# Choosing 128 of 4096 tokens for each of 48 experts: one wide search, or many short ones and a second one over their results

## The chip, the cores and the metric

The kernel runs on one core of a Trainium2 chip. The metric is the device time of one execution in microseconds (us), as the median of several runs. The core has five engines that work side by side and wait for each other through semaphores: TensorE (matrix products, PE in the profile), VectorE (DVE), ScalarE (ACT), GpSimd (POOL) and SyncE (SP). SP issues most transfers between main memory and the on-chip memory; GpSimd issues those whose rows are given by a list of indices.

## The reference

The program is a chain of four blocks over 16 sequences of 256 tokens, 128 numbers each (4096 tokens, float32). Every block is half a feed-forward step, an attention step and the same half feed-forward step again, each on the layer-normed input and added to x. The change concerns the feed-forward step of block 2, a mixture of experts in which the experts choose tokens:

```python
def _L2_ffn_ref(x, Wr, W1, b1, W2, b2):
    CAP_FACTOR = 1.5
    ...
    cap = int(CAP_FACTOR * T / E)            # 128 tokens for each of E = 48 experts
    logits = xf @ Wr.T                       # T = 4096
    vals, idx = jax.lax.top_k(logits.T, cap)
    w = jax.nn.softmax(vals, axis=-1)
    xg = xf[idx]
    h = jax.nn.gelu(jnp.einsum('ecd,esdm->ecsm', xg, W1) + b1[:, None], approximate=False)
    y = jnp.einsum('ecsm,esmk->ecsk', h, W2) + b2[:, None]
    y = y.reshape(E, cap, D) * w[..., None]
    out = jnp.zeros_like(xf).at[idx.reshape(-1)].add(y.reshape(-1, D))
    return out.reshape(orig_shape)
```

So each expert takes the 128 tokens with its highest logits, weights them by a softmax over these 128 values, and adds its results to the tokens' rows. The step runs twice, before and after the attention of block 2.

## The kernel before

The list `steps` at the end of `macaron_kernel` runs twelve steps in order: ffn0, attn0, ffn0, ffn1, attn1, ffn1, ffn2, attn2, ffn2, ffn3, attn3, ffn3. x, its normed copy xn (tokens on partitions) and the transposed normed copy xnT stay on chip throughout. A framework orders the instructions of a step by its own estimate of when each is ready, by program order among those that are, and may take an instruction early into the step before. Two things limit that. `pin` ties an instruction to the last pinned one on the same engine, so that pinned instructions of an engine keep program order. An `If` on a value read from memory is a unit: nothing moves into it, out of it or across it.

**Pieces.** `norm_piece(c)` (through `roots`) norms 512 tokens: statistics and an inverse root in some 22 small VectorE operations, then four ScalarE activations that write xn. `turn_piece(c)` transposes these four tiles on TensorE and copies them into xnT. Both are pinned. The plain `layernorm` does all of x at once without pins.

**ffn2.** It stores xn to `xn_dram` for the gathers, clears one accumulator in main memory and stores x to the other. The router product (L1275) puts the logits of 64 experts (48 real) on partitions 0 to 63 for tokens 0 to 2047 and on 64 to 127 for the rest, 2048 to a partition. The search (L1282 to L1286) makes 16 rounds: MAX8 finds the eight highest of a row, FIND_INDEX8 their places, MATCH_REPLACE8 overwrites them. `expert_lists` turns the lists of both halves so that slots lie on partitions; half 1 is reversed, so that a comparison slot by slot (L1294) leaves the best 128. Softmax weights follow (L1304 to L1315).

The expert loop then takes each of the 48 experts: GpSimd gathers 128 rows of 512 bytes into xg (L1328, three buffers), TensorE transposes (L1335), VectorE copies (L1337), four products h (L1340), four Gelu activations (L1344), the bias and four products y (L1346, L1348), the weighting into ys (L1352), and a scatter that adds ys to the accumulator (L1353). Weights come on SP for four experts at a time. `gather_acc` sums the accumulators into x.

**ffn1**, 64 experts with eight per token, comes before the first ffn2. Its second call has `normed=True`. After its own routing and search it reads a flag under an `If` (L1068, L1069), then loops over eight groups of eight experts; each group has four gathers (L1087) and four scatters (L1127) on GpSimd. Six of the groups also call `shared(c)`, which completes x for 512 tokens that no expert can touch unless the flag is set. Only the first 1024 tokens' x waits for `gather_acc`, and a second `If` (L1135) follows it. In the first call `norm_piece` and `turn_piece` of the six later pieces run inside this loop.

**attn2** is a pipeline written out by hand over 22 values of s, nearly all pinned, one sequence per s. In a step come `keys(s)` (L1421), `rest(s-2)` (L1570), `renorm` in odd steps, `stand` (L1481, and L1484 on VectorE), `through` (L1496), `divisors` (L1515), `queries`, `divide`, `gather`, `put(s-1)` (L1559) and norm pieces. The results of `gather`'s totals, `stand` and `put` share one memory bank, the pool `pm` with one buffer.

Of the kernel before, what the change touches and what calls it, by code (L numbers as in the profile page):

```python
# [9 lines left out]
F32 = mybir.dt.float32  # L10
# [30 lines left out]
GE2 = 4  # L41

# [28 lines left out]
def macaron_kernel(ctx: ExitStack, tc: tile.TileContext, I: dict, out: bass.AP):  # L71
# [93 lines left out]
    def iota(name, pattern, base, mult, n):  # L165
        t = const.tile([P, n], F32, name=name)
        G.iota(t, pattern=pattern, base=base, channel_multiplier=mult, allow_small_or_imprecise_dtypes=True)
        return t
# [21 lines left out]

    left = iota("left", [[-P, NT]], T, -1, NT)
# [14 lines left out]
    xn_dram = dram.tile([T + PAD, D], F32, name="xn_dram")  # L206

# [3 lines left out]
    SP.dma_start(out=xn_dram[T:, :], in_=zeros[:, :D])  # L211
    for a in acc:
        SP.dma_start(out=a[T:, :], in_=zeros[:, :D])
# [84 lines left out]
    def norm_piece(c):  # L298

        t0 = 4 * c  # L300
        less, r = roots(x[:, t0 : t0 + 4, :], LN_EPS)
        for j in range(4):
            pin(
                S.activation(  # L304
                    xn[:, t0 + j, :], x[:, t0 + j, :], AF.Identity, bias=less[:, j : j + 1], scale=r[:, j : j + 1]
                )
            )
# [606 lines left out]
    def ffn1(call, normed):  # L914
# [8 lines left out]
        with tc.tile_pool(name=f"f1r{call}", bufs=1) as rp, tc.tile_pool(name=f"f1w{call}", bufs=2) as wp, tc.tile_pool(  # L923
# [148 lines left out]
            with tc.tile_pool(name=f"f1h{call}", bufs=1, space=PSUM) as ph:  # L1072
                n = GE1 // 2
                for g in range(E1 // GE1):

                    if g < NT // 4 - FIRST // 4:
                        c = FIRST // 4 + g
                        if not normed:
                            norm_piece(c)
                            turn_piece(c)  # L1080
                        shared(c, ph)
                    wgu, wd = early.pop(g, None) or weights(g)
# [51 lines left out]
            gather_acc(acc, 0, FIRST)  # L1134
            rv = nc.values_load(more[0:1, 0:1], min_val=0, max_val=P * E1)  # L1135
            with tc.If(rv > 0):
                gather_acc(acc, FIRST, NT, add=True)

# [119 lines left out]
    def ffn2(call, normed):  # L1258
        if not normed:
            layernorm()  # L1260
        SP.dma_start(out=xn_dram[:T, :].rearrange("(j p) d -> p j d", p=P), in_=xn)
# [4 lines left out]
        with tc.tile_pool(name=f"f2r{call}", bufs=1) as rp, tc.tile_pool(name=f"f2w{call}", bufs=2) as wp, tc.tile_pool(  # L1266
            name=f"f2t{call}", bufs=3
        ) as tp3:
            lgT = rp.tile([P, T // 2], F32, name="f2_lgT")
            with tc.tile_pool(name=f"f2p{call}", bufs=2, space=PSUM) as pr:  # L1270
                for c in range(4):
                    lp = pr.tile([P, 512], F32, tag="lp", name="f2_lp")
                    for h in range(2):
                        t0 = h * (T // 2) + c * 512
                        PE.matmul(  # L1275
                            lp[64 * h : 64 * h + 64, :], W["f2_rw"], xnT[:, t0 : t0 + 512], start=True, stop=True
                        )
                    S.copy(lgT[:, c * 512 : (c + 1) * 512], lp)
            vals = rp.tile([P, CAP2], F32, name="f2_vals")
            where = rp.tile([P, CAP2], U32, name="f2_where")  # L1280
            for r in range(CAP2 // 8):
                cut = slice(8 * r, 8 * r + 8)  # L1282
                V.max(out=vals[:, cut], in_=lgT)  # L1283
                V.max_index(out=where[:, cut], in_max=vals[:, cut], in_values=lgT)  # L1284
                if r < CAP2 // 8 - 1:
                    V.match_replace(out=lgT, in_to_replace=vals[:, cut], in_values=lgT, imm_value=LOWEST)  # L1286
            wf = rp.tile([P, CAP2], F32, name="f2_wf")
            V.tensor_copy(wf, where)
            V.tensor_scalar(wf[64:P, :], wf[64:P, :], float(T // 2), None, ALU.add)
            lv = expert_lists(vals, "f2v")  # L1290
            li = expert_lists(wf, "f2i")

            pick = rp.tile([P, 64], F32, name="f2_pick")
            V.tensor_tensor(pick, lv[:, :64], lv[:, 64:], ALU.is_ge)  # L1294
            top = rp.tile([P, 64], F32, name="f2_top")
            V.tensor_tensor(top, lv[:, :64], lv[:, 64:], ALU.max)
            tokf = rp.tile([P, 64], F32, name="f2_tokf")
            V.tensor_tensor(tokf, li[:, :64], li[:, 64:], ALU.subtract)
            V.tensor_tensor(tokf, tokf, pick, ALU.mult)
            idx = rp.tile([P, 64], I32, name="f2_idx")  # L1300
            V.tensor_tensor(idx, tokf, li[:, 64:], ALU.add)  # L1301

            tpa = pst.tile([P, 512], F32, tag="tp", name="f2_tpa")
            PE.transpose(tpa[:64, :P], top, ident)  # L1304
            nm = rp.tile([64, 1], F32, name="f2_nm")
            V.tensor_reduce(nm, tpa[:64, :P], AX.X, ALU.max, negate=True)
            ex = rp.tile([64, P], F32, name="f2_ex")
            sm = rp.tile([64, 1], F32, name="f2_sm")
            S.activation(ex, tpa[:64, :P], AF.Exp, bias=nm, accum_out=sm)
            V.reciprocal(sm, sm)  # L1310
            V.tensor_scalar(ex, ex, sm, 0.5, ALU.mult, ALU.mult)
            tpb = pst.tile([P, 512], F32, tag="tp", name="f2_tpb")
            PE.transpose(tpb[:, :64], ex, ident[:64, :64])
            wgt = rp.tile([P, 64], F32, name="f2_wgt")
            V.tensor_copy(wgt, tpb[:, :64])  # L1315

            with tc.tile_pool(name=f"f2h{call}", bufs=2, space=PSUM) as ph:
                for g in range(E2 // GE2):
                    w1 = wp.tile([P, GE2, S2, M2], F32, tag="w1", name="f2_w1")
                    SP.dma_start(out=w1.rearrange("p e s m -> p (e s m)"), in_=I["f2_w1"][g])  # L1320
                    w2 = wp.tile([P, GE2, S2, K2], F32, tag="w2", name="f2_w2")
                    SP.dma_start(out=w2.rearrange("p e s k -> p (e s k)"), in_=I["f2_w2"][g])
                    b2 = wp.tile([1, GE2, D], F32, tag="b2", name="f2_b2")
                    SP.dma_start(out=b2.rearrange("p e d -> p (e d)"), in_=I["f2_b2"][g : g + 1, :])
                    for i in range(GE2):
                        e = g * GE2 + i
                        xg = tp3.tile([P, D], F32, tag="xg", name="f2_xg")
# [3 lines left out]
                            in_=xn_dram,  # L1331
# [3 lines left out]
                        PE.transpose(tp[:, :P], xg, ident)  # L1335
# [16 lines left out]
                        V.tensor_scalar(ys, y, wgt[:, e : e + 1], None, ALU.mult)  # L1352
# [10 lines left out]
    def attn2():  # L1363

        NP2 = H2 // 2
        with tc.tile_pool(name="a2", bufs=2) as ap, tc.tile_pool(name="a2w", bufs=1) as wp, tc.tile_pool(
# [219 lines left out]
            for s in range(BATCH + 6):  # L1586
# [24 lines left out]
                if s >= 5 and s % 2 and (s - 5) // 2 < pieces:  # L1611
                    norm_piece((s - 5) // 2)


    def ffn3(call, last):
# [176 lines left out]
        lambda: ffn2(0, False), attn2, lambda: ffn2(1, True),  # L1792
        lambda: ffn3(0, False), attn3, lambda: ffn3(1, True),
    ]
    banks = None
    for step in steps:
        if step in (attn0, attn3):
            if banks is not None:
                banks.close()
                banks = None  # L1800
            if step is attn3:
                late_pool.append(ctx.enter_context(tc.tile_pool(name="late", bufs=2)))
            step()
        else:
            if banks is None:
                banks = ExitStack()
                pst.pool, pst.tag = banks.enter_context(tc.tile_pool(name="pst", bufs=2, space=PSUM)), "tp"
            step()
    banks.close()
# [90 lines left out]
```

## Time and profile before

| | |
|---|---|
| median of 3 runs | 3072.5 us (3072.13 to 3077.36) |
| the profiled execution | 3084.44 us, span 3082.7 us |
| TensorE, VectorE, ScalarE, GpSimd busy | 2349.2, 1567.7, 1002.9, 758.2 us |
| mean granted TensorE clock | 0.841 |
| first ffn2: x complete, search, first gather, last scatter | 1168.8; 1194.0 to 1305.4; 1309.0; 1475.2 us |
| attn2: last output product ends | 1843.1 us |
| second ffn2: search, last scatter | 1868.1 to 1979.5; 2147.8 us |
| ffn1, second call: first gather, last scatter | 1044.5; 1152.8 us |

A group line reads: line, engine, operation, out<-in, shapes, count, busy us, mean ns, and the idle time of that engine just before with what ended it. A time-line row begins with its start and duration. A row of a table by stretches gives, for each engine, busy us and instructions, then the granted clock as a share of full speed, the busy share of the transfer engines and GB/s. An `f_` in a name stands for any of the prefixes f0_ to f3_.

### The profile page before, as it was taken

The page shows a single profiled execution, that of the slowest core. Times are in us where ns is not written, and L with a number is a line of the kernel's source. Part 1 is how long each engine was busy: PE and PEld are TensorE (multiplying, and loading weights), DVE is VectorE, ACT ScalarE, POOL GpSimd, SP SyncE. Part 2 cuts the span into 40 slices and gives each one's busy share as a digit, 9 for nine tenths or more (in the row PEclk, how much of TensorE's full clock was granted, in tenths as well). Part 3 has the DMA queues.
Part 4 walks back from the last instruction along what each step waited for, and adds up shares of the span by engine and source line. Part 5 has one row for each costly group of instructions (what it writes and reads, how often), then busy time and mean ns, then how long its engine had stood idle before and what let it go on. Part 6 is the DMA issues. An engine that isn't in the chain of part 4 may idle for free.

```text
span 3082.7 us, 44329 instructions
## 1 busy us (share of the span) xinstructions
PE 2349.2 (76%) x16626; PEld 1776.8 (58%) x16626; DVE 1567.7 (51%) x3989; ACT 1002.9 (33%) x2211; POOL 758.2 (25%) x673
## 2 busy tenths in 40 slices
PE   5885896883745561099799981298899989999999
PEld 4773555772545350088566650187588745556887
DVE  5336664336447527911245449711555566653553
ACT  1222221221225201033444531033444445654443
POOL 1550000551630270067100001176111100002111
PEclk9997886995869765567899995567999989999999
DMA  4842232453530354045300002055100022220000
GB/s 138 257 136 63 79 100 76 148 150 88 134 67 8 95 108 142 0 119 128 89 1 1 1 1 89 26 125 128 30 1 1 2 43 59 61 63 13 8 11 11
DMA packets 197271, 215.68 MB, mean 70 GB/s; under 512 B 37329, under 2 KB 162290, under 8 KB 193682
## 3 DMA queue, kind: packets, MB, share of 16 engines
q1 hardware_dynamic: 161978, 177.63, 19.0%
q0 software_dynamic: 35072, 35.16, 6.8%
q8 instruction: 133, 2.18, 0.3%
q14 instruction: 88, 0.72, 0.1%
HBM read 142.76 MB, written 61.31 MB: 66 GB/s over the span
## 4 chain that ended last, share of the span: by engine, by line
PE 46%; DVE 10%; DMA 2%; ACT 1%; issue 1%; POOL 1%; another core or an unknown queue 0%; POOLq 0%; DVEq 0%; ACTq 0%; SPq 0%
PE f_m L1683 12%; PE f_h L1340 4%; PE a_s L822 4%; PE f_y L1348 2%; DVE f_where L1284 2%; DVE f_vals L1283 2%; DVE f_lgT L1286 2%; PE a_po L564 2%; PE a_t L822 2%; PE a_op L1559 2%; PE a_gp L1469 2%; PE f_yp L1741 2%; PE a_qp L1432 2%; PE a_kp L1421 2%; PE f_z L1663 2%; PE f_z L1664 2%
## 5 line engine op out<-in xcount | busy, mean ns | idle before, releaser
L471 PE MATMUL f_h<-f_xsT,f_w 128*128 128x256 f32 x736 | 189.8, 396 | 34.4 <-ACT f_sg L473 27.7
L826 DVE TENSOR_REDUCE a_nm<-a_s 128x4 f32<-128x1024 f32 x128 | 156.3, 1224 | 100.4 <-PE a_t L822 89.1
L304 ACT ACTIVATE xn<-x,ln_less,ln_r 128x128 f32<-128x128 f32 x256 | 105.8, 482 | 290.7 <-DVE ln_less L295 280.2
L445 POOL DMA_INDIRECT f_xs<-xn_dram,f_src x92 | 90.6, 985 | 371.1 <-DVE f_past L418 290.2
L474 DVE SCALAR_TENSOR_TENSOR f_hs<-f_h,f_b1s,f_sg 128x256 f32<-128x256 f32 x184 | 88.1, 482 | 180.3 <-issue 97.3
L822 PE MATMUL a_t<-a_q,a_k 32*128 32x256 f32 x1024 | 173.3, 424 | 3.5 <-ACT a_e L830 3.5
L1344 ACT ACTIVATE f_hs<-f_h,w_f_b 128x128 f32<-128x128 f32 x384 | 109.6, 369 | 203.0 <-PE f_h L1340 172.4
L830 ACT ACTIVATE a_e<-a_t 128x512 f32<-128x512 f32 x256 | 139.1, 594 | 104.5 <-PE a_t L822 104.5
L1328 POOL DMA_INDIRECT f_xg<-xn_dram,f_idx x96 | 96.5, 1005 | 304.0 <-DVE f_idx L1301 257.4
L471 PEld LDWEIGHTS f_h<-f_xsT,f_w 128*128 128x128 f32 x736 | 134.0, 197 | 62.5 <-ACT f_sg L473 34.4
L1340 PE MATMUL f_h<-f_xgT,f_w 128*128 128x128 f32 x768 | 165.7, 364 | 0.0
L896 PE MATMUL f2v_tp<-ident,f2v_turned 128*128 128x128 f32 x2 | 0.9, 475 | 212.2 <-DVE f2v_turned L893 212.2
L1352 DVE TENSOR_SCALAR f_ys<-f_y,f_wgt 128x128 f32<-128x128 f32 x96 | 33.6, 350 | 250.5 <-PE f_y L1348 182.2
L1353 POOL DMA_INDIRECT acc<-f_ys,f_idx x96 | 150.8, 1571 | 40.0 <-issue 24.0
L822 PE MATMUL a_s<-a_k,a_q 32*128 32x256 f32 x1024 | 155.2, 431 | 2.3 <-DVE a_nm L826 1.6
L473 ACT ACTIVATE f_sg<-f_h,f_b1s 128x256 f32<-128x256 f32 x184 | 84.9, 474 | 214.5 <-PE f_h L471 182.2
L1348 PEld LDWEIGHTS f_y<-f_w,f_hs 128*128 128x128 f32 x768 | 139.6, 238 | 15.9 <-ACT f_hs L1344 4.3
L1348 PE MATMUL f_y<-f_w,f_hs 128*128 128x32 f32 x768 | 146.0, 290 | 2.1 <-ACT f_hs L1344 2.0
L312 PE MATMUL ln_tp<-ident,xn 128*128 128x128 f32 x256 | 56.0, 321 | 111.7 <-ACT xn L304 101.1
L1340 PEld LDWEIGHTS f_h<-f_xgT,f_w 128*128 128x128 f32 x768 | 136.7, 257 | 0.7 <-issue 0.4
L1702 ACT ACTIVATE f_nh<-f_c,w_f_sh 128x256 f32<-128x256 f32 x192 | 86.9, 500 | 127.7 <-DVE f_c L1721 103.2
L896 PEld LDWEIGHTS f2v_tp<-ident,f2v_turned 128*128 128x128 f32 x2 | 0.4, 182 | 212.7 <-DVE f2v_turned L893 212.7
(398 smaller groups left out, 5756.0 us busy)
## 6 DMA issues: line engine op xcount, KB each, us to landing
f_w<-in_f_w SPq DMA_DIRECT2D x24, 1024.0 KB
f_w<-in_f_w SPq DMA_DIRECT2D x46, 512.0 KB
f_w<-in_f_w SPq DMA_DIRECT2D x70, 256.0 KB
a_ud<-a_u SPq DMA_DIRECT2D x32, 512.0 KB
f_wgu<-in_f_wgu SPq DMA_DIRECT2D x16, 768.0 KB
acc<-zeros SPq DMA_DIRECT2D x14, 512.0 KB
acc_t<-acc SPq DMA_DIRECT2D x14, 512.0 KB
f_wd<-in_f_wd SPq DMA_DIRECT2D x16, 384.0 KB
```

Of the source, the lines that this page charges most:

```text
L304: S.activation(xn[:, t0 + j, :], x[:, t0 + j, :], AF.Identity, bias=less[:, j : j + 1], scale=r[:, j : j + 1])
L445: G.indirect_dma_start(out=xs[:, i, :], out_offset=None, in_=xn_dram, in_offset=bass.IndirectOffsetOnAxis(ap=src[:, s : s + 1], axis=0),)
L471: pin(PE.matmul(h[:, k, :], w1[:, cc * P : (cc + 1) * P], xsT, start=True, stop=True))
L822: pin(PE.matmul(ps[:, c, :], sta[:, c * P : (c + 1) * P], mov, start=True, stop=True))
L826: pin(V.tensor_reduce(m, sp, AX.X, ALU.max, negate=True))
L830: pin(S.activation(e, tp, AF.Exp, scale=scale))
L1328: G.indirect_dma_start(out=xg, out_offset=None, in_=xn_dram, in_offset=bass.IndirectOffsetOnAxis(ap=idx[:, e : e + 1], axis=0),)
L1340: PE.matmul(h[:, s, :], w1[:, i, s, :], xgT, start=True, stop=True)
L1344: S.activation(hs[:, s, :], h[:, s, :], AF.Gelu, bias=W["f2_b1"][:, col : col + 1])
L1348: PE.matmul(y[:, s * K2 : (s + 1) * K2], hs[:, s, :], w2[:, i, s, :], start=False, stop=(s == S2 - 1))
L1353: G.indirect_dma_start(out=acc2[e % 2], out_offset=bass.IndirectOffsetOnAxis(ap=idx[:, e : e + 1], axis=0), in_=ys, in_offset=None, comput ...
L1683: PE.matmul(dst[:, n, :], sta[:, k, n * P : (n + 1) * P], mov[:, k, :], start=first and n == 0 and k == 0, stop=n == 1 and k == 1, skip_gr ...
```

## The change

The search of ffn2 is done in two levels, the first of them outside ffn2.

`pick(c)` handles 512 tokens, two sequences: router products put 256 logits of each expert on each half of the partitions, four more products leave the same logits with tokens on partitions (kept in `f2_lt`), and four rounds find the 32 best of each row of 256 with their places. Values, places and `T` minus the token's number are kept for all eight pieces. It also stores the piece's xn to a new table `xl_dram`, whose rows have 192 numbers. `choose(c)` is norm_piece, turn_piece and pick. ffn1's second call runs `choose` for pieces 2 to 7 in its loop and for 0 and 1 after `gather_acc`; the `If` now stands ahead of that sum in both calls. attn2 runs `pick` in the even steps from s = 6.

ffn2 loses its layernorm, the xn store and the wide search. It issues the weights of two groups, then makes twelve rounds over the 256 candidates of a row (no more than 96 per half), turns the lists, finds the 128th value as a limit and the highest one, and makes twelve rounds over `T` minus the token's number, masked by the limit, to get the token numbers. Beside this `exponentials` writes exp(logit - highest) for every token and expert into the last 64 columns of the table: four additions on GpSimd, four activations, four stores. The sums of the chosen exponentials give `share`. A check counts the chosen; if it fails for any expert, an `If` runs the old wide search.

In the expert loop a gathered row has 768 bytes, and ys is the product times the row's own column `D + e` times `share`.

```diff
@@ ffn1
+                    if normed and 1 <= g <= NT // 4 - FIRST // 4:
+                        choose(FIRST // 4 + g - 1)
                     wgu, wd = early.pop(g, None) or weights(g)
...
-            gather_acc(acc, 0, FIRST)
             rv = nc.values_load(more[0:1, 0:1], min_val=0, max_val=P * E1)
             with tc.If(rv > 0):
                 gather_acc(acc, FIRST, NT, add=True)
+                if normed:
+                    for c in range(FIRST // 4, NT // 4):
+                        choose(c)
+            gather_acc(acc, 0, FIRST)
+            if normed:
+                for c in range(FIRST // 4):
+                    choose(c)
@@ new
+    def pick(c):
+        f2_cv, f2_ci, f2_kv, f2_lt, pair, f2_lg = chosen
+        SP.dma_start(
+            out=xl_dram[c * 512 : (c + 1) * 512, :D].rearrange("(j p) d -> p j d", p=P), in_=xn[:, 4 * c : 4 * c + 4, :]
+        )
+        tp = pst.tile([P, 512], F32, tag="tp", name="f2_lp")
+        for h in range(2):
+            t0 = c * 512 + h * SEQ
+            pin(
+                PE.matmul(
+                    tp[64 * h : 64 * h + 64, :SEQ],
+                    W["f2_rw"],
+                    xnT[:, t0 : t0 + SEQ],
...
+        for i in range(4):
+            cut = slice(SEQ + 64 * i, SEQ + 64 * i + 64)
+            pin(PE.matmul(tp[:, cut], tok(4 * c + i), W["f2_rw"], start=True, stop=True, skip_group_check=True))
+        lg = f2_lg[c % 2]
+        pin(S.copy(lg, tp[:, :SEQ]))
+        pin(S.copy(f2_lt[:, 4 * c : 4 * c + 4, :], tp[:, SEQ:].rearrange("p (j e) -> p j e", e=64)))
+        for r in range(C2 // 8):
+            cut = slice(8 * r, 8 * r + 8)
+            pin(V.max(out=f2_cv[:, c, cut], in_=lg))
+            pin(V.max_index(out=f2_ci[:, c, cut], in_max=f2_cv[:, c, cut], in_values=lg))
+            if r < C2 // 8 - 1:
+                pin(V.match_replace(out=lg, in_to_replace=f2_cv[:, c, cut], in_values=lg, imm_value=LOWEST))
+        pin(V.tensor_copy(f2_kv[:, c, :], f2_ci[:, c, :]))
+        pin(V.tensor_scalar(f2_kv[:, c, :], f2_kv[:, c, :], -1.0, base8[:, c : c + 1], ALU.mult, ALU.add))
+
+    def choose(c):
+        norm_piece(c)
+        turn_piece(c)
+        pick(c)
@@ attn2, at the end of a step
                 if s >= 5 and s % 2 and (s - 5) // 2 < pieces:
                     norm_piece((s - 5) // 2)
+                if s >= 6 and s % 2 == 0 and (s - 6) // 2 < pieces:
+                    pick((s - 6) // 2)
@@ ffn2
-        SP.dma_start(out=xn_dram[:T, :].rearrange("(j p) d -> p j d", p=P), in_=xn)
...
+            def exponentials(least, pool):
...
+                for c in range(0, NT, 8):
+                    cut = f2_lt[:, c : c + 8, :]
+                    ex = pool.tile([P, 8, 64], F32, tag="ex", name="f2_ex", bufs=2)
+                    G.tensor_tensor(ex, cut, bc(mb, 1, 8), ALU.add)
+                    S.activation(ex, ex, AF.Exp)
+                    SP.dma_start(
+                        out=xl_dram[c * P : (c + 8) * P, D:].rearrange("(j p) d -> p j d", p=P), in_=ex
+                    )
...
+                for r in range(HALF2 // 8):
+                    cut = slice(8 * r, 8 * r + 8)
+                    V.max(out=vals[:, cut], in_=work)
+                    if r < HALF2 // 8 - 1:
+                        V.match_replace(out=work, in_to_replace=vals[:, cut], in_values=work, imm_value=LOWEST)
+                lv = expert_lists(vals, "f2v")
...
+                V.scalar_tensor_tensor(key, cv, lim[:, 0:1], kv, ALU.is_ge, ALU.mult)
...
+                exponentials(least, qp)
...
+                for r in range(HALF2 // 8):
+                    cut = slice(8 * r, 8 * r + 8)
+                    V.max(out=first[:, cut], in_=key)
+                    if r < HALF2 // 8 - 1:
+                        V.match_replace(out=key, in_to_replace=first[:, cut], in_values=key, imm_value=0.0)
+                li = expert_lists(first, "f2i")
...
+            rv = nc.values_load(again[0:1, 0:1], min_val=0, max_val=P * P)
+            with tc.If(rv > 0):
...
-                        xg = tp3.tile([P, D], F32, tag="xg", name="f2_xg")
+                        xg = tp3.tile([P, XW], F32, tag="xg", name="f2_xg")
...
-                        PE.transpose(tp[:, :P], xg, ident)
+                        PE.transpose(tp[:, :P], xg[:, :D], ident)
...
-                        V.tensor_scalar(ys, y, wgt[:, e : e + 1], None, ALU.mult)
+                        V.tensor_scalar(ys, y, xg[:, D + e : D + e + 1], share[:, e : e + 1], ALU.mult, ALU.mult)
```

## The prediction

> **What bounds the kernel now.** I read the page's chain of work first, then the groups by shape, then stretches of the time line around the two searches.
>
> ```profile
> PE 46%; DVE 10%; DMA 2%; ACT 1%; issue 1%; POOL 1%; another core or an unknown queue 0%; POOLq 0%; DVEq 0%; ACTq 0%; SPq 0%
> ```
>
> TensorE holds most of the chain; VectorE's 10% are largely the two searches of ffn2. Their groups by shape (count, total us and mean ns, idle before):
>
> ```profile
> L1283 DVE MAX8 f_vals<-f_lgT 128x8 f32<-128x2048 f32 x32 | 73.4, 2295 | 10.5 <-ACT f_lgT L1278 9.5
> L1284 DVE FIND_INDEX8 f_where<-f_vals,f_lgT 128x8 uint32<-128x2048 f32 x32 | 73.1, 2284 | 0.0
> L1286 DVE MATCH_REPLACE8 f_lgT<-f_vals,f_lgT 128x2048 f32<-128x2048 f32 x30 | 68.3, 2276 | 0.0
> L999 DVE MAX8 f_first<-f_keyT 128x8 f32<-128x512 f32 x16 | 11.1, 694 | 0.6
> L1001 DVE MATCH_REPLACE8 f_keyT<-f_first,f_keyT 128x512 f32<-128x512 f32 x14 | 9.5, 675 | 0.0
> ```
>
> The first three are the search: idle before them is nearly nothing, so each runs back to back, 1194.0 to 1305.4 us in the first ffn2 and 1868.1 to 1979.5 in the second, and nobody else works. The last two give the price per width: (2295 - 694) / 1536 = 1.04 ns an element.
>
> The first search starts 25 us after x is complete (1168.8), the second 25 us after the last output matmul of attn2 (1843.1); first gathers start at 1309.0 and about 1983. These two stretches, 140 us each, are what the change attacks.
>
> **Small search, level one.** At 256 elements MAX8 is 2295 - 1792 x 1.04 = 0.43 us, FIND_INDEX8 0.42, MATCH_REPLACE8 0.41. A round at 2048 repeats every 7.11 us, 0.26 above its three operations, so a round at 256 is 1.51. Three whole rounds, one without replacement (1.0) and two small conversions (0.4): 5.9 us of VectorE for each of 8 pieces, per call. A norm_piece in front is 3.8 us of VectorE, four ACT rows and four transposes. From its end to the start of the search lie 4.9 us with TensorE warm (2.7 to the copied xnT, as at the end of attn2, then six router matmuls 1.35, copy 0.45, hand-overs), 6.3 cold. The 256-wide ACT copy is put at the 0.37 us of attn0's and the 0.50 of ffn3's.
>
> **In ffn1's second call** six such pieces (9.7 us of VectorE each, 58 us) go into the expert loop. Its cover is POOL, whose transfers are issued one after the other. The same loop in the first call carries the norm pieces already:
>
> ```profile
> core 0: us, PE busy (x) PEld busy (x) DVE busy (x) ACT busy (x) POOL busy (x), PEclk, DMA share, GB/s
> 760.70:875.00 114.30, 76.23 (x512) 58.22 (x512) 48.47 (x167) 22.21 (x45) 81.44 (x64) 0.71 0.49 108
> 1044.50:1154.40 109.90, 75.11 (x488) 58.93 (x486) 29.67 (x44) 10.76 (x16) 81.91 (x64) 0.67 0.52 112
> ```
>
> 18.8 us more of VectorE cost 4.4 us, a share of 0.23. For 58 us that makes **+14 us**; the bounds are 0 (VectorE reaches only 88 of 110 us) and 30 (every search holding one 5 us group step). Each piece also puts a 256 KB row store on SP, ahead of expert weights; that is in the bounds.
>
> The tail is serial: pieces 0 and 1 wait for x at 1168.8, and the pins put norm 1 behind search 0. 2 x (3.8 + 6.3 + 5.9) = 32 us, until 1200.8. Putting the branch before gather_acc moves SP's loads perhaps 2 us later and saves 1.3 at its exit: nothing.
>
> **In attn2** the first seven searches are pinned between put of an even step and rest of the odd one. The steady odd step:
>
> ```profile
> 1635.88 3.60 PE L1421 MATMUL a_kp<-w_a_wk,xnT 128*128 128x512 f32 x8
> 1639.32 0.95 PE L1481 MATMUL a_ks<-a_halves,a_tot 128*128 128x2 f32 x8
> 1640.20 1.97 PE L1496 MATMUL a_mp<-a_vf,a_g 128*64 128x128 f32 x32
> 1642.10 1.07 PE L1515 MATMUL a_dp<-a_q,a_sums 128*32 128x256 f32 x16
> ```
> ```profile
> 1636.08 0.42 DVE L1570 TENSOR_TENSOR a_r<-a_op,xn 128x256 f32<-128x256 f32 x1 [2.42 <-PE a_op L1559]
> 1640.31 0.26 DVE L1484 TENSOR_TENSOR a_sums<-a_ks,a_mask 128x16 f32<-128x16 f32 x2
> ```
>
> TensorE has no gap here. a_op and a_ks share the one bank of pool pm, so a_ks waits for a_r; a_dp waits for a_sums, which stands behind a 3.8 us renorm on VectorE. Counted from 1635.88: router matmuls to 1.35, search 2.1 to 8.0, a_r to 8.4, renorm to 12.2, a_sums to 12.5, a_dp at 12.6 instead of 6.2. So each search costs 6.4 us though VectorE is half idle. Five fall in the steady part (steps 6 to 14): **+32 us**. The other three lie in the tail.
>
> Stalls of 3.9 us also touch the clock. Around the end of attn2:
>
> ```profile
> 1832.00:1834.00 2.00, 0.92 (x16) 0.72 (x16) 1.02 (x1) 0.00 (x0) 0.00 (x0) 1.00 0.00 0
> 1834.00:1836.00 2.00, 1.08 (x8) 0.86 (x4) 1.69 (x3) 0.00 (x0) 0.00 (x0) 0.57 0.02 4
> 1836.00:1838.00 2.00, 2.00 (x6) 0.94 (x5) 0.79 (x2) 0.00 (x0) 0.00 (x0) 0.50 0.00 0
> 1838.00:1840.00 2.00, 2.00 (x7) 1.13 (x6) 0.00 (x0) 0.00 (x0) 0.00 (x0) 0.50 0.00 0
> 1840.00:1842.00 2.00, 2.00 (x15) 2.00 (x15) 0.00 (x0) 0.00 (x0) 0.00 (x0) 0.72 0.00 0
> ```
>
> The granted clock halves for some 6 us after about 4 us of half-idle work, a loss of 3 us. The Trainium skill ("TensorE: Matmul & The Clock Gate", Part 1) says that a wholly idle free-running window of about 3.4 us drops the clock and a busy one restores it. By the rule a 3.9 us stall rarely contains a window: 0 to 2 us over the five. By the row: 5 x 3 = 15. I take **+8**.
>
> Tail, from put's end at 1843.1 (shifted by the above): search 5 to 8.0, rest and renorm to 12.2, ACT and POOL complete x(7) at 16.6, norm 6 to 18 (its small operations wait for POOL's two, as they do now), search 6 from 23 to 29; norm 7 is pinned behind it, to 32.8; search 7 from 37.6 to **43.5**.
>
> **Level two and the branch.** Copy 0.3; 12 rounds of MAX8 and MATCH_REPLACE8 at 256: (0.43 + 0.41 + 0.15) x 12 less the last replacement = 11.3 (the 0.15 is what the 512-wide round, 1.51, has above its two operations). Two turned copies, transpose, list copy: 1.5, as from 1305.4 to 1306.9 now. Best, transpose, two reductions, one matmul, limit: 2.0. Keys, `taken` and the start of the exponentials: 1.1. Second 12 rounds 11.3, lists 1.5, indices 0.5, then sums, counts and the check with three small matmul round trips: 4. Together 33.4 us. Beside it run POOL's four additions (1.26 each by its 128x512 rows), ACT's Exp and the table's four stores. A store of this shape, 256 KB from f_wt, issued at 1026.9 with 512 KB behind it, was over by 1032. So the table lands some 6 us before the branch; uncovered, it would add a few us. The branch itself is priced in ffn1 now:
>
> ```profile
> 1040.20 0.15 DVE L1029 CAST f_more<-f_cp 1x1 int32<-1x1 f32 x1
> 1044.52 1.02 POOL L1087 DMA_INDIRECT f_xg<-xw_dram,f_idx  x1 [74.15 <-DVEq L1069]
> ```
>
> 4.2 us from the flag to the first gather. So 37.6 in all.
>
> First call: 32 + 37.6 = 69.6 against 140.2: **-70.6**. Second: 43.5 + 37.6 = 81.1 against 140: **-58.9**.
>
> **The experts.** Now a row tile is free after its transpose; then it is held until f_ys reads its weight column, with three tiles as before. Today a gather runs 4 to 5 experts ahead of f_ys (29 gathers issued, 24 weighted, at 1401); after, three. POOL's own pace, from its lines:
>
> ```profile
> L1328 POOL DMA_INDIRECT f_xg<-xn_dram,f_idx x96: 939/1013/1027, 1309.0 to 2136.0; - x96
> L1353 POOL DMA_INDIRECT acc<-f_ys,f_idx x96: 1552/1572/1635, 1321.1 to 2147.8; - x96
> ```
>
> With 0.3 us before each, 3.2 us; the phase runs at 167 / 48 = 3.48. The new loop for three experts: scatter in front 2.2, gather 1.0, landing 1.65 when quiet to 4 under weight loads, transpose to f_ys 3.7 warm and 4.9 cold: 8.5 to 12 us, 2.8 to 4.0 an expert. When quiet it hides behind POOL, otherwise not, and TensorE's gaps invite the slow clock, where the start of the phase (1313 to 1340, clock 0.50) runs at 4.28. Bounds 0 and +1.0 us; I take +0.37 x 96 = **+36**. The longer row (768 B) costs no issue time: ffn1's gathers of that length are 0.98 us.
>
> Setup at the start, under 1 us, and ffn3's 10 us of POOL preparation, which the branch moves into POOL's first wait for row tiles, are put at nothing; uncovered, up to 10.
>
> **Sum.** -70.6 - 58.9 + 14 + 32 + 8 + 36 = -39.5, say -40. It is made against a profiled execution of 3084.4 us (span 3082.7), 12 above the median of 3072.5; the difference is carried over to the median: **3032 us**. Its own range, with the terms moved halfway to their ends, is 3008 to 3056.
>
> **Rivals.** *The insertions hide* (22%): ffn1 +4, attn2 +15, clock 0, experts +10. Idle VectorE and POOL's pace speak for it; the pinned order speaks against. -129.5 + 29 = -100, 2972.
>
> *The row tiles throttle the experts* (24%): at three tiles TensorE stays on the slow clock, where it needs 4.28 us an expert by itself, and the gather round trip adds 0.3: 4.6, +1.12 x 96 = +107 in place of +36, 3103. It decides from +0.79 us an expert, 4.27, where the other terms (-75.5) are used up. For it: the clock alternates between 0.5 and 1.0 already. Against: in the slow stretch TensorE, not POOL, is the bound, and extra waits overlap with it.
>
> *The short search is refused* (5%): the fallback would run both times, about 115 us each, near 3260. With the reference's own logits no piece of 256 holds more than 24 of an expert's 128 (limit 31), no half more than 81 (limit 96). Only a limit that isn't bit-equal after three passes through TensorE could trip it.
>
> **How the numbers follow.** The likeliest case has 49%. Range 2966 to 3108: it leaves out the fallback, the lower part of the second case and the upper of the third. A change under 0.2% (6 us) can't be told from none here. Faster: 48 of the likeliest and 22, 70%; same: 1 and 2 of the third case, 3%; slower: its other 22 and 5, 27%.
>
> **What would show it.** Right: first gather about 70 us after x in the first call; a_dp 6 us later after each search; ffn1's loop near 124 us; f_xg waiting for DVE f_ys; experts near 3.85 us. Wrong: a stall-free odd step, 2048-wide searches still present, or first gathers waiting for the table's stores.

## The result, and the profile after

The changed kernel is slower: median 3182.3 us (3179.95 to 3188.92, 4 runs) against 3072.32 us (3070.9 to 3077.36, 4 runs), a ratio of 1.0358 with a 95% interval of 1.0338 to 1.0379. The prediction was 3032 us. The profiled execution took 3180.47 us, span 3178.6, mean granted clock 0.803 (0.841 before). The check on the short search did not fail in either call: no instruction of the wide search runs.

The chain of work that ended last, from the page of the changed kernel:

```profile
PE 32%; DVE 2%; DMA 1%; issue 1%; ACT 1%; POOL 0%; SPq 0%; ACTq 0%; POOLq 0%; DVEq 0%
```

VectorE's 10% are down to 2%: the search is off the chain. The groups by shape show its new price, and something else (count, total us and mean ns, idle time of the engine just before and what ended it; lines between are left out at the dots):

```profile
L1519 PE MATMUL f_h<-f_xgT,f_w 128*128 128x128 f32 x768 | 247.7, 464 | 1.5 <-DVE f_xgT L1516 1.5
...
L1532 POOL DMA_INDIRECT acc<-f_ys,f_idx x96 | 151.0, 1572 | 200.9 <-DVE f_ys L1531 191.2 <-DVE f_xgT L1516 8.2 <-issue 1.4
...
L1531 DVE TENSOR_SCALAR f_ys<-f_y,f_xg,f_share 128x128 f32<-128x128 f32 x96 | 39.4, 410 | 279.2 <-PE f_y L1527 279.2
...
L1317 DVE MAX8 f_cv<-f_lg 128x8 f32<-128x256 f32 x64 | 27.3, 427 | 87.9 <-ACT f_lg L1313 86.4
L1318 DVE FIND_INDEX8 f_ci<-f_cv,f_lg 128x8 uint32<-128x256 f32 x64 | 26.8, 419 | 0.0
...
L1320 DVE MATCH_REPLACE8 f_lg<-f_cv,f_lg 128x256 f32<-128x256 f32 x48 | 19.6, 408 | 0.0
```

The 256-wide operations cost 427, 419 and 408 ns. But VectorE stood idle for 86.4 us in all ahead of the first MAX8 of the 16 pieces, waiting for the logits' copy; GpSimd stood idle for 191.2 us in all ahead of the experts' scatters, waiting for the weighting; and the products h take 464 ns in the mean. The same two lines of the kernel before, with 11.7 us of waiting for the weighting:

```profile
L1340 PE MATMUL f_h<-f_xgT,f_w 128*128 128x128 f32 x768 | 165.7, 364 | 0.0
L1353 POOL DMA_INDIRECT acc<-f_ys,f_idx x96 | 150.8, 1571 | 40.0 <-issue 24.0 <-DVE f_ys L1352 11.7 <-DVE f_xgT L1337 3.8
```

A table of phases puts the time in its place. Each border is an event of the trace: first gather of the second ffn1 ("ffn1"), x complete, first expert gather, last scatter, first key product of attn2, last output product, first gather, last scatter, first product of ffn3, end.

| phase, us | before | after | difference | predicted |
|---|---|---|---|---|
| start to second ffn1's first gather | 1044.5 | 1037.3 | -7.2 | 0 |
| ffn1: first gather to x complete | 124.2 | 172.1 | +47.9 | +14 |
| x complete to first expert gather | 140.3 | 66.8 | -73.5 | -70.6 |
| experts, first call | 167.7 | 241.9 | +74.2 | +18 |
| to attn2's first key product | 18.7 | 19.4 | +0.7 | 0 |
| attn2: to the last output product | 347.7 | 383.2 | +35.5 | +40 |
| to the first gather, second call | 140.1 | 79.7 | -60.4 | -58.9 |
| experts, second call | 166.2 | 245.5 | +79.3 | +18 |
| to the end | 933.4 | 932.7 | -0.7 | 0 |

They sum to +95.8 us, the difference of the two spans. The medians differ by 110 us, since the profiled execution of the kernel before was 12 us above its median. Two terms carry the miss: the experts (118 us over the prediction) and ffn1 (34 us).

**The experts.** A stretch of the second call, in the table by stretches (PE, PEld, DVE, ACT, POOL busy with counts, granted clock, transfer share, GB/s):

```profile
2075.00:2100.00 25.00, 23.92 (x98) 20.62 (x97) 3.32 (x10) 5.72 (x20) 12.84 (x10) 0.50 0.39 90
2100.00:2125.00 25.00, 24.22 (x98) 21.00 (x98) 3.72 (x11) 5.72 (x20) 13.05 (x11) 0.50 0.42 112
```

TensorE is busy 96% of the time and its clock stays at half. The trace's clock changes only at multiples of 3.41 us; of the 143 such windows in the two expert phases 141 are at half (49 of 98 before).

**ffn1.** One group's start on TensorE and VectorE, from the time line:

```profile
1099.58 1.12 PE L1300 MATMUL f_lp<-xnT,w_f_rw 128*64 128x256 f32 x4 [0.68 <-ACT xnT L324]
1100.63 1.97 PE L1311 MATMUL f_lp<-w_f_rw,xnT 128*128 128x64 f32 x8
1102.40 1.06 PE L1106 MATMUL f_xtp<-ident,f_xg 128*128 128x128 f32 x4
```
```profile
1103.05 0.43 DVE L1317 MAX8 f_cv<-f_lg 128x8 f32<-128x256 f32 x1 [6.36 <-ACT f_lg L1313]
1103.51 0.69 DVE L1108 COPY f_xgT<-f_xtp 128x512 f32<-128x512 f32 x1
```

The group's rows had been gathered long before. Their transposes (L1106) stand on TensorE behind the router products, which wait for the turned xnT, which waits for the norm; their copy (L1108) stands on VectorE behind the first MAX8, which has waited 6.36 us for the logits. The next norm then stands behind this group's weighting. So norm, turn, router, copy and the group's own work form one serial chain of some 21.5 us (the scatters of the fourth, fifth and sixth group begin at 1114.7, 1136.0 and 1157.6), where the kernel before repeats every 12.8 to 13.7.

**attn2**, an odd step:

```profile
1735.77 1.41 PE L1660 MATMUL a_ks<-a_halves,a_tot 128*128 128x2 f32 x8 [3.33 <-DVE a_r L1749]
1737.11 3.22 PE L1675 MATMUL a_mp<-a_vf,a_g 128*64 128x128 f32 x32
1740.26 1.07 PE L1694 MATMUL a_dp<-a_q,a_sums 128*32 128x256 f32 x16
```
```profile
1735.14 0.24 DVE L1322 TENSOR_SCALAR f_kv<-f_kv,base 128x32 f32<-128x32 f32 x1
1735.29 0.42 DVE L1749 TENSOR_TENSOR a_r<-a_op,xn 128x256 f32<-128x256 f32 x1
```

a_ks waits 3.33 us for a_r, which stands behind the search on VectorE (f_kv is the search's last operation). Most of a_ks and a_mp then runs at half clock (4.6 us for 2.9), as the next window of 3.41 us shows:

```profile
1732.89:1736.30 3.41, 0.53 (x5) 0.54 (x5) 3.24 (x14) 0.18 (x1) 0.00 (x0) 1.00 0.01 2
1736.30:1739.71 3.41, 3.41 (x29) 3.39 (x30) 2.77 (x20) 0.33 (x1) 0.00 (x0) 0.50 0.00 0
```

### The profile page after: what moved, and what is told of

It is laid out like the page before. It is cut to its first block, busy times and chain, and to the rows that moved or that the text cites. A ratio compares the mean times of both kernels' runs of the same rounds, so it can differ in the third digit from the quotient of the medians.

```text
span 3178.6 us, 45443 instructions
## 1 busy us (share of the span) xinstructions
PE 2534.8 (80%) x16808; PEld 1919.9 (60%) x16808; DVE 1492.3 (47%) x4375; ACT 1026.6 (32%) x2270; POOL 770.8 (24%) x693
## 3 DMA queue, kind: packets, MB, share of 16 engines
q1 hardware_dynamic: 170666, 179.82, 18.6%
## 5 line engine op out<-in xcount | busy, mean ns | idle before, releaser
L1519 PE MATMUL f_h<-f_xgT,f_w 128*128 128x128 f32 x768 | 247.7, 464 | 1.5 <-DVE f_xgT L1516 1.5
L315 ACT ACTIVATE xn<-x,ln_less,ln_r 128x128 f32<-128x128 f32 x288 | 119.0, 482 | 378.0 <-DVE ln_less L306 364.8
L323 PE MATMUL ln_tp<-ident,xn 128*128 128x128 f32 x288 | 68.0, 337 | 202.1 <-ACT xn L315 191.6
L1527 PEld LDWEIGHTS f_y<-f_w,f_hs 128*128 128x128 f32 x768 | 187.0, 323 | 31.1 <-ACT f_hs L1523 28.8
L1532 POOL DMA_INDIRECT acc<-f_ys,f_idx x96 | 151.0, 1572 | 200.9 <-DVE f_ys L1531 191.2
L1519 PEld LDWEIGHTS f_h<-f_xgT,f_w 128*128 128x128 f32 x768 | 190.5, 329 | 8.5 <-issue 5.8
L1527 PE MATMUL f_y<-f_w,f_hs 128*128 128x32 f32 x768 | 187.4, 369 | 7.3 <-ACT f_hs L1523 7.2
L323 PEld LDWEIGHTS ln_tp<-ident,xn 128*128 128x128 f32 x288 | 40.2, 156 | 234.2 <-ACT xn L315 213.5
L1531 DVE TENSOR_SCALAR f_ys<-f_y,f_xg,f_share 128x128 f32<-128x128 f32 x96 | 39.4, 410 | 279.2 <-PE f_y L1527 279.2
L1140 POOL DMA_INDIRECT acc<-f_ys,f_idy x64 | 100.8, 1574 | 84.6 <-DVE f_ys L1137 54.6
L833 PEld LDWEIGHTS a_s<-a_k,a_q 32*128 32x128 f32 x1024 | 91.1, 198 | 47.3 <-issue 34.0
```

Of the source, the lines that this page charges most:

```text
L315: S.activation(xn[:, t0 + j, :], x[:, t0 + j, :], AF.Identity, bias=less[:, j : j + 1], scale=r[:, j : j + 1])
L323: pin(PE.transpose(tp[:, i * P : (i + 1) * P], xn[:, 4 * c + i, :], ident))
L833: pin(PE.matmul(ps[:, c, :], sta[:, c * P : (c + 1) * P], mov, start=True, stop=True))
L1140: G.indirect_dma_start(out=acc_two[e % 2], out_offset=bass.IndirectOffsetOnAxis(ap=idy[:, e : e + 1], axis=0), in_=ys[:, i, :], in_offset= ...
L1519: PE.matmul(h[:, s, :], w1[:, i, s, :], xgT, start=True, stop=True)
L1527: PE.matmul(y[:, s * K2 : (s + 1) * K2], hs[:, s, :], w2[:, i, s, :], start=False, stop=(s == S2 - 1))
```

## The experiments

They ran on more than one chip. The kernel before, run beside each, took from 3030 to 3085 us in the median there, and the work ahead of the second ffn1, the same in all of them but for the place of one branch, from 1001 to 1053 us; so a whole time is given as a ratio to the kernel before on the same chip, and causes are read from the phases.

The theory at this point: a row tile that is held until the weighting throttles the experts, with the clock as part of it; in ffn1 the chain ahead of a group's own work costs, not VectorE's busy time.

**Six row tiles.**

```diff
-xg = tp3.tile([P, XW], F32, tag="xg", name="f2_xg")
+xg = tp3.tile([P, XW], F32, tag="xg", name="f2_xg", bufs=6)
```

> The changed kernel with six row tiles for the experts in place of three. Theory of the held tiles: a tile that is kept until the weighting makes each gather wait for a weighting three experts back, TensorE gets a small gap in each expert, and with these gaps its clock stays at half for the whole phase (5.0 us an expert). Six tiles let the gathers run ahead again: 3.5 us an expert, 96 x 1.5 = 144 us less than 3182, so about 3038, granted clock mostly above 0.5 in both phases. Rival, the long rows: 768 bytes a row at the same rate give no relief, so 3175 to 3185. Rival, the weighting with two scalars or the clock alone: also no change.

Ratio 0.9822 (0.9779 to 0.9866); expert phases 170.5 and 166.7 us, all other phases as after. One argument of one line turns the changed kernel from 3.6% slower to 1.8% faster than the kernel before. Its groups by shape:

```profile
L1519 PE MATMUL f_h<-f_xgT,f_w 128*128 128x128 f32 x768 | 161.5, 368 | 0.0
...
L1532 POOL DMA_INDIRECT acc<-f_ys,f_idx x96 | 152.0, 1583 | 52.3 <-DVE f_ys L1531 23.8 <-issue 17.8 <-DVE f_xgT L1516 8.0
```

The product h is back at 368 ns and GpSimd's wait for the weighting fell from 191.2 to 23.8 us. Rows are still 768 bytes long and the weighting still has two scalars: neither was the cause.

**The kernel before, with its tile held.**

```diff
-V.tensor_scalar(ys, y, wgt[:, e : e + 1], None, ALU.mult)
+V.tensor_scalar(ys, y, xg[:, 0:1], wgt[:, e : e + 1], ALU.mult, ALU.mult)
```

> The kernel before, with 512-byte rows and its three tiles, but the weighting also multiplies by the first number of each gathered row, so that the tile is held until then (the output is therefore another one; no work is left out). Held tiles: 4.5 to 5.0 us an expert in place of 3.48, 96 x 1.0 to 1.5, so 3170 to 3220, and gathers and scatters wait for the weighting. Long rows as the cause: no change, 3070 to 3080.

Ratio 1.0483 (1.0430 to 1.0537); expert phases 240.6 and 237.9 us. Nothing else of the change is in this kernel, and its groups by shape are those of the changed kernel:

```profile
L1340 PE MATMUL f_h<-f_xgT,f_w 128*128 128x128 f32 x768 | 247.1, 463 | 1.5 <-DVE f_xgT L1337 1.5
...
L1353 POOL DMA_INDIRECT acc<-f_ys,f_idx x96 | 151.4, 1577 | 201.5 <-DVE f_ys L1352 191.6 <-DVE f_xgT L1337 8.5 <-issue 1.4
```

Holding the tile is enough by itself. How one tile goes round, as medians over the middle experts of a phase, from the starts in the trace:

| us | before | after | before, held | four tiles |
|---|---|---|---|---|
| gather to its transpose | 6.1 to 6.4 | 4.7 to 4.8 | 4.7 | 7.3 |
| transpose to end of copy | 0.75 | 0.75 to 0.78 | 0.75 | 0.75 |
| copy to weighting | 7.3 to 7.4 | 6.7 | 6.7 | 8.0 |
| weighting to scatter | 3.1 to 3.8 | 0.69 | 0.69 | 0.69 |
| scatter to the gather that reuses the tile | - | 1.88 | 1.88 | 1.90 |
| expert to expert (mean) | 3.4 | 5.0 | 5.0 | 4.65 |

The held round is 4.75 + 0.76 + 6.71 + 0.69 + 1.88 = 14.8 us. For three tiles that is 4.93 us an expert, and 5.0 was measured. The long part is from the transpose to the weighting. In the changed kernel one row is transposed at 2079.42 and weighted at 2086.24, and in between TensorE also takes the next row (2082.70) and products of the experts on both sides:

```profile
2079.42 0.45 PE L1514 MATMUL f_tp<-ident,f_xg 128*128 128x128 f32 x1
2082.70 0.42 PE L1514 MATMUL f_tp<-ident,f_xg 128*128 128x128 f32 x1
```
```profile
2086.24 0.41 DVE L1531 TENSOR_SCALAR f_ys<-f_y,f_xg,f_share 128x128 f32<-128x128 f32 x1 [2.78 <-PE f_y L1527]
```

**The weight columns copied out at once**, with three tiles (an earlier form, which copied one column, did not compute the step; its times are not used):

```diff
+cols = tp3.tile([P, XW - D], F32, tag="cols", name="f2_cols", bufs=6)
+V.tensor_copy(cols, xg[:, D:])
...
-V.tensor_scalar(ys, y, xg[:, D + e : D + e + 1], share[:, e : e + 1], ALU.mult, ALU.mult)
+V.tensor_scalar(ys, y, cols[:, e : e + 1], share[:, e : e + 1], ALU.mult, ALU.mult)
```

> As the copy of one weight column, but all 64 columns of the row are copied into a small tile when it arrives (96 copies of about 0.2 us): the row tile is free early, with three tiles. Held tiles: 168 to 180 us a phase in place of 242 and 246. Long rows or the clock for another reason: 235 to 246.

Phases 171.1 and 176.8 us, ratio 0.9894 (0.9855 to 0.9934): the same recovery without a larger row buffer.

**Four row tiles:**

```diff
-xg = tp3.tile([P, XW], F32, tag="xg", name="f2_xg")
+xg = tp3.tile([P, XW], F32, tag="xg", name="f2_xg", bufs=4)
```

> The changed kernel with four row tiles for the experts. Held tiles: a fourth tile lets a gather run one expert further ahead. If the loop over the tiles alone set the pace, 5.0 x 3/4 = 3.75 us an expert, so 240 us a phase would become about 180. If TensorE's gaps and its half clock set it, the step is not in proportion: either the gaps stay and with them the half clock (225 to 245 us), or they go and POOL's pace is back (165 to 175).

Phases 225.7 and 229.1 us, ratio 1.0271 (1.0218 to 1.0323). The second branch came true, but not as worded. Three of its stretches, same columns as above:

```profile
1292.00:1317.00 25.00, 25.00 (x106) 22.22 (x105) 3.51 (x10) 5.72 (x20) 13.65 (x11) 0.50 0.47 120
1317.00:1342.00 25.00, 25.00 (x103) 21.80 (x102) 4.21 (x12) 6.35 (x23) 13.49 (x11) 0.50 0.45 111
1342.00:1367.00 25.00, 25.00 (x103) 22.09 (x103) 3.51 (x10) 6.23 (x22) 14.79 (x12) 0.50 0.40 90
```

TensorE has no gap, its matmul row is full (the profile models the ends of matmuls, so this row may hide small gaps), and still the clock stays at half: here TensorE at half clock is the bound (4.65 us an expert) and the round of the tiles, 18.6 us for four, only follows it. The weight loads, the second pair of numbers, fill 88%. That made a new theory: what lifts the clock is dense TensorE work, which the matmul row does not measure. If so, more work should make the phase shorter.

**Four unread products more for each expert**, with three tiles and with four:

```diff
 for s in range(S2):
     PE.matmul(h[:, s, :], w1[:, i, s, :], xgT, start=True, stop=True)
+for s in range(2):
+    PE.matmul(spare, w1[:, i, s, :], xgT, start=True, stop=True)
...
+for s in range(2, 4):
+    PE.matmul(spare, hs[:, s, :], ident, start=True, stop=True)
 ys = tp3.tile([P, D], F32, tag="ys", name="f2_ys")
```

> The same four extra products with four row tiles, where TensorE showed no idle time but weight loads filled only 84 to 92 per cent of most stretches. Dense work lifts the clock: 170 to 200 us a phase in place of 226 and 229, granted clock above 0.7. Extra work is simply paid at half clock: 275 to 300 us.

Measured 188.4 and 189.0 us, 37 and 40 less than without the extra products (ratio 1.0026, 1.0003 to 1.0049). Two stretches:

```profile
1272.00:1302.00 30.00, 30.00 (x235) 27.42 (x234) 6.03 (x17) 10.23 (x36) 22.23 (x17) 1.00 0.61 165
1302.00:1332.00 30.00, 29.16 (x218) 26.87 (x216) 5.32 (x15) 9.15 (x33) 20.34 (x16) 0.94 0.50 122
```

The clock is up. With four tiles the clock, not the round of the tiles, was the bound.

> The changed kernel with three row tiles and four extra products of 128 x 128 for each expert, whose results nobody reads: two behind the four products h, two behind the products y (nothing is left out). If the lack of dense TensorE work is what keeps the clock at half, the extra work fills some of the gaps, the clock goes up at times and the phase gets shorter although there is more to do: 190 to 235 us in place of 242 and 246. If the clock stays at half whatever is added, the extra products are simply paid: 4 x 0.26 to 0.4 us x 48, 290 to 320 us.

Neither: 237.8 and 248.6 us, though in the first phase the clock rose to between 0.74 and 0.95 in stretches of 25 or 30 us (ratio 1.0340, 1.0294 to 1.0386). The round of three tiles stayed at 15 to 16 us, with the extra products now in it. So with three tiles a higher clock bought this way does not help: the round is the bound. What three tiles would take at full clock without the extra products is not shown.

**ffn1 staggered:** norm in one group, turn in the next, search in the one after.

```diff
-if normed and 1 <= g <= NT // 4 - FIRST // 4:
-    choose(FIRST // 4 + g - 1)
+late = FIRST // 4 + g - 1
+if normed and FIRST // 4 <= late - 2 < NT // 4:
+    pick(late - 2)
+if normed and FIRST // 4 <= late - 1 < NT // 4:
+    turn_piece(late - 1)
+if normed and FIRST // 4 <= late < NT // 4:
+    norm_piece(late)
...
+if normed:
+    pick(NT // 4 - 1)
```

> The changed kernel, but in the loop of the second ffn1 a piece is normed in one group of experts, transposed in the next and searched in the one after; the last search follows the loop. Theory of the chain: norm, transposes, router products and copy stand on three engines one behind the other ahead of the group's own transposes, and that chain (some 8 us a group, six groups) is the 48 us that the phase got longer. Taken apart it is 30 to 40 us shorter: 3142 to 3152. Rival, VectorE's added 58 us of work or the shared memory banks: the same work stays in the loop, so less than 10 us gained, 3172 to 3182.

Ratio 1.0276 (1.0229 to 1.0323); ffn1 153.5 us, 18.6 less, half of what was expected. While gathers last, the step from scatter to scatter fell to 12.6 to 16.6 us, near GpSimd's own pace. The last two groups, with no gathers to cover them, took 18.5 each (7.8 in the kernel before).

**Only norm and turn in the loop**, the six searches behind it (with six tiles):

```diff
-choose(FIRST // 4 + g - 1)
+norm_piece(FIRST // 4 + g - 1)
+turn_piece(FIRST // 4 + g - 1)
...
+for c in range(FIRST // 4, NT // 4):
+    pick(c)
```

> The changed kernel with six row tiles, and in the second ffn1 only norm and transposes of the six pieces in the loop, their router products and searches after it, ahead of the sum of the accumulators. Theory of the chain: norm and transposes alone cost the loop 5 to 10 us, as in the first call of ffn1, and the six searches of 6 us come after it, partly under the last scatters and the accumulator loads: from first gather of ffn1 to first gather of the experts 218 to 230 us, against 239 in the changed kernel. Rival, VectorE's work or the norm part alone is what costs: 236 us or more.

154.7 us to complete x and 221.4 to the first expert gather, inside the first range; ratio 0.9775 (0.9722 to 0.9828). The same search work costs 17.5 us less behind the loop than in it (221.4 against 238.9): the place costs, not the work alone.

**Three edits together:** six tiles, the stagger, and in attn2 the router products behind `queries`, the search behind `divide`.

```diff
+if picked:
+    pick_logits((s - 6) // 2)
 if 1 <= s < BATCH + 1:
     divide(s - 1)
+if picked:
+    pick_search((s - 6) // 2)
...
-if s >= 6 and s % 2 == 0 and (s - 6) // 2 < pieces:
-    pick((s - 6) // 2)
```

> The changed kernel with three edits: six row tiles; the staggered pieces in ffn1; and in attn2 the router products of a search moved behind queries of the same even step and its VectorE part behind divide, so that it runs while TensorE does the totals and put, and no longer stands ahead of rest of the odd step. Phases: experts 170 and 167 us and ffn1 from first gather to complete x 154, as in the single runs. Attn2 from first key product to last put: theory of the order, the 3.3 us wait of a_ks and the half clock after it go, 1.75 us of router products stay: 355 to 365 in place of 383. Rival, the searches cost VectorE or ScalarE time that attn2 lacks wherever they stand: 378 to 386. Whole: 0.972 to 0.980 of the kernel before by the first, 0.980 to 0.986 by the second.

Ratio 0.9727 (0.9689 to 0.9765). The tiles held (166.9, 163.9) and ffn1 took 144.7, but attn2 376.5 us, outside the range of the theory. TensorE's and ScalarE's rows show where the wait went:

```profile
1587.31 2.74 PE L1616 MATMUL a_kp<-w_a_wk,xnT 128*128 128x512 f32 x6
1593.59 1.54 PE L1616 MATMUL a_kp<-w_a_wk,xnT 128*128 128x512 f32 x2 [3.54 <-ACT a_k L1618]
```
```profile
1591.41 1.65 ACT L315 ACTIVATE xn<-x,ln_less,ln_r 128x128 f32<-128x128 f32 x4 [6.89 <-DVE ln_less L306]
1592.96 1.53 ACT L1618 ACTIVATE a_k<-a_kp 128x512 f32<-128x512 f32 x3
```

The search now stands ahead of the next norm on VectorE; ScalarE's norm, behind it, stands ahead of the key activations, and those free the banks that the key products need. The 3.3 us moved from a_ks to a_kp.

**The attn2 search in two halves** of two rounds, each behind `divisors`, where VectorE waits about 3.2 us for TensorE:

```diff
 divisors(s - 1)
+if 7 <= s < BATCH and s % 2:
+    pick_search((s - 7) // 2, range(2))
+if 8 <= s < BATCH + 1 and s % 2 == 0:
+    pick_search((s - 8) // 2, range(2, 4))
...
-if picked:
+if picked and s >= BATCH:
     pick_search((s - 6) // 2)
```

> The version with six row tiles, staggered ffn1 and moved attn2 searches, with one more edit: in the steady steps of attn2 the VectorE part of a search is cut in two halves of two rounds, one behind divisors of the odd step, one behind divisors of the next even step, where VectorE waits about 3.2 us for TensorE. Theory: in the version before this one the search pushed the norm of the next piece back, and with it ScalarE's norm ahead of the key activations (TensorE waited 3.5 us for them). Attn2 then needs 348 + 5 x 1.75 = 357 us, up to 362; whole 0.964 to 0.970 of the kernel before. Rival, any added VectorE or ScalarE work in a step is paid: 372 to 380, 0.972 to 0.976.

Attn2 352.1 us, 4.4 above the kernel before: the searches are hidden. Ratio 0.9628 (0.9591 to 0.9665).

**Three of ffn1's searches behind the loop** on top of that (pieces 5, 6 and 7):

```diff
-    if normed and FIRST // 4 <= late - 2 < NT // 4:
+    if normed and FIRST // 4 <= late - 2 < 5:
         pick(late - 2)
...
-    pick(NT // 4 - 1)
+    for c in range(5, NT // 4):
+        pick(c)
```

> The version with halved attn2 searches, and in the second ffn1 only the first three staggered searches stay in the expert loop; those of pieces 5, 6 and 7 follow it, ahead of the accumulator sums. In the staggered runs the last two groups of experts, which have no gathers left, took 17.5 to 18.5 us each from scatter to scatter (7.8 in the kernel before). Theory of the order: what stands ahead of a group's own copy and weighting on VectorE is paid in full once GpSimd has no gathers left to cover it. Then ffn1 from first gather to complete x falls from 147 to 135 to 141 us, and from first gather to first gather of the experts from 213 to 203 to 209, as the moved searches run while the accumulators are loaded. Rival, the same searches are paid wherever they stand: 213 or more.

140.8 us to complete x, 207.3 to the first expert gather, as the order would have it. Ratio 0.9614 (0.9582 to 0.9647), not told apart from the run before by its whole time. Both are faster than the kernel before by nearly 4%, and the change's idea was sound: its search saves 134 us, and 237 us of losses around it (48 in ffn1, 36 in attn2, 154 in the experts) hid that.

## Why the prediction was wrong

**The search** was right, in its parts too: -70.6 and -58.9 predicted, -73.5 and -60.4 measured. Two serial pieces took 31.9 us (32), attn2's tail 45.5 (43.5), level two and branch 34.9 and 34.2 (37.6). The check's flag was written at 1274.0 and the first gather started at 1276.2, 2.2 us instead of the 4.2 taken from ffn1.

**attn2** was right in sum: +35.5 for 32 + 8, in part by luck. Two steps take 49.2 to 50.8 us where they took 42.4. The parts were others than listed: 3.33 us of waiting and 1.75 of router products in each of the five, about 25 us instead of 32, since renorm stayed hidden behind the slowed a_mp; and about 10 of half clock (an estimate: the clock stood at 0.50 for 27.3 us of attn2, 6.8 before, and half of that is lost). It fell in each of the five steps, behind a window of 3.41 us in which TensorE was idle for 1.4 to 3.2 us. So the rule of the wholly idle window, from which the prediction had 0 to 2 us, does not fit these falls; the row of the kernel before, from which it had 15, came nearer.

**The experts** were the step that failed, as the prediction put it: "8.5 to 12 us, 2.8 to 4.0 an expert", +36 with a bound of +1.0 us an expert. It measured +153.5, 1.6 us an expert. The mechanism was seen (a tile held, three of them, TensorE's gaps and the clock); the rival that named it gave +107 and was itself 46 us short. The mis-sized term is "transpose to f_ys 3.7 warm and 4.9 cold". Between a transpose and its weighting TensorE works through parts of the neighbouring experts too, as its instructions stand interleaved: 7.5 us, and the trace of the kernel before already had 8.1 for it (0.75 + 7.3). The row also waits behind them before its transpose, 4.75 us after the gather started, where 2.7 to 5 were allowed for. So the round was 14.8 us, not 8.5 to 12. The clock was taken as an average over slow and fast stretches; it was slow in 141 of 143 windows. And the argument against the rival, that in the slow stretch TensorE is the bound and extra waits overlap with it, took that stretch as a short one and its 4.28 us an expert as fixed. With four tiles TensorE is the bound without a gap and takes 4.65 us at half clock throughout; the runs with extra products there show that the clock itself was worth at least 37 and 40 us a phase. Of the 1.6 us an expert that leaves, as an estimate from the phases (3.48 before, 4.74 with four tiles, 5.08 with three), 1.3 for TensorE at half clock and 0.3 for having three tiles instead of four.

**ffn1** failed at "a share of 0.23": VectorE's extra busy time scaled by what the norm pieces had cost in the first call, with a bound of +30. It measured +47.9, about 8 us for each of the six groups. The bound assumed "every search holding one 5 us group step" and so counted VectorE's part alone. The wait in front of the search, 6.4 us for ScalarE's part of the norm, transposes, router products and copy, was not counted, though these stand in pinned order on three engines ahead of the group's own work. The stagger alone gives back 18.6 us; the stagger and the late searches together bring the phase to 140.8, near the 138 that the prediction had; what stays of the 16.6 us above the kernel before is not traced further.

## What to carry to other kernels

A buffer's price is its round, from the gather to the last reader, divided by the number of buffers: when an edit moves the last reader, add up the new round from the trace's starts, with the neighbouring items' work that stands between in each engine's queue, before trusting that a faster part hides it. Work put into a loop costs by the chain that it puts ahead of the loop's own instructions in each engine's order; its busy time says little. When such a change disappoints, look at the phases one by one: here one argument of one line decided the sign.

## What the runs showed of the hardware

A full matmul row does not mean a full clock. With four tiles TensorE's matmul row was at 100% for 175 us (1267 to 1442) at clock 0.50. The Trainium skill ("TensorE: Matmul & The Clock Gate", Part 1) says that one busy window of about 3.4 us brings the clock up, so measurement and page differ if busy means that row. The weight loads tell better. In the windows of 3.41 us of the expert phases, over eleven runs (all but the two with extra products and the one not used), a window at half clock whose weight loads filled at least 99% was followed by full clock in 146 of 182 cases; one with under 96% in 9 of 655. A full matmul row was followed by it in 150 of 589. Three windows of the kernel before, from its table by stretches:

```profile
1332.53:1335.95 3.42, 3.42 (x17) 3.13 (x15) 0.50 (x2) 0.00 (x0) 2.59 (x2) 0.50 0.34 97
1335.95:1339.36 3.41, 3.41 (x17) 3.41 (x17) 0.35 (x1) 1.14 (x4) 2.59 (x2) 0.50 0.29 38
1339.36:1342.77 3.41, 3.41 (x28) 3.09 (x27) 1.10 (x4) 1.14 (x4) 1.57 (x2) 1.00 0.29 34
```

In the first the matmuls are full and the weight loads at 92%, and the clock stays; in the second both are full, and the next is at 1.00. The falls look the same from the other side. In these phases the clock fell 152 times, once behind a window in which TensorE was idle throughout or nearly so, and 72 times behind one whose matmul row was at least 95% full:

```profile
1424.70:1428.11 3.41, 3.41 (x28) 3.09 (x27) 0.75 (x3) 1.51 (x6) 2.51 (x2) 1.00 0.90 318
1428.11:1431.53 3.42, 3.42 (x19) 3.42 (x18) 0.35 (x1) 1.14 (x4) 2.65 (x3) 0.50 0.66 143
```

These are relations found in these traces, and the extra products, which raised density and clock together, agree with them; what the chip counts is not shown. The consequence was measured: with four tiles, 192 unread products a phase made it 37 and 40 us shorter.
